# Storing an image once in four row bands and gathering it by rows of taps, and making two rank masks once, in a one-core kernel with four layers

## Chip, cores and metric

The kernel runs on one core of one Trainium2 chip, in one launch. Its metric is the device time in microseconds (us). The kernel before took 10140.57 us (median of three runs, 10136.91 to 10153.51). One more execution was profiled. It took 10153.48 us, of which 10151.7 us lie between its first and its last instruction.

## What is computed

The reference is a stack of four layers on a float32 tensor x of shape (4, 128, 64, 64): four images of 128 channels. Only layer 0 is touched, and in it only the part that ends with the order of the patches:

```
x_adapted = gn(x)
feat = gelu(dwconv2d(x_adapted, conv1_w, conv1_b))     # 3x3, each channel alone
ca = feat.mean((2, 3))
ca = sigmoid(maximum(ca @ ca1_w.T, 0.0) @ ca2_w.T)
feat = feat * ca[:, :, None, None]
feat = gelu(dwconv2d(feat, conv2_w, conv2_b))          # 3x3, each channel alone
scores = sigmoid(einsum('bchw,oc->bohw', feat, head_w)[:, 0] + head_b[0])
pv = var(x_adapted, axis=1, ddof=1)
final_scores = 0.7 * scores + 0.3 * sigmoid(pv * 10.0)
sm = final_scores.reshape(B, Hp, PS, Wp, PS).mean((2, 4)).reshape(B, Hp * Wp)
idx = argsort(-sm, axis=1)                             # 256 patches of 4x4 pixels
```

The patches in this order, with a position embedding added and normalized, go through a projection, a causal convolution, a selective scan over the 4096 positions (16 states, 256 inner channels) and a projection back. Layer 1 is a 3x3 convolution over all channels. Layers 2 and 3 are an attention and a small mixture of experts each, and the change does not touch them.

## The kernel before

`layers01` holds layers 0 and 1. It has three stages, each with its own pools.

Stage one prepares image 0: it runs the generator `in_order(0)` alone, on engines that are otherwise empty. Stage two is `scan`: it goes through the four images, eight chunks of 512 positions each and eight pairs of states (g) in each chunk. For each g, VectorE (DVE) makes `hs` (L901) and runs four scans (L912) with `decay` factors that ScalarE (ACT) computes just ahead (L908), in two half turns of two scans each. GpSimd (POOL) multiplies `hs` by `c_sb` (L916), which SyncE (SP) loads from DRAM (L870), and TensorE (PE) adds it up (`y_ps`). Beside this, `scan` advances `in_order(b + 1)` by one turn (one `yield`) in every half turn, so that image b + 1 is prepared while image b is scanned. In the last image's scan, the finished images go through layer 1 instead (`end`). Stage three finishes the last image.

Stage one is ordered by the tile framework's scheduler. In stage two the order on each engine is the order in which the program writes the instructions (`manual_schedule`). All engines take their instructions in order; so a wait at the head of one engine's queue holds up what is behind it. Operations handed to `later` are written at the next `flush`, which is half a turn later.

All DMAs of the kernel are issued by SP. In the built program a DMA also waits, before it is issued, until the DMA eight places ahead of it on SP has landed: there are eight semaphores, used in rotation.

How one image gets its two depthwise convolutions (lines of the kernel before):

- `groupnorm_fill` (L209) writes eight rows of `xp`, the normalized image with a border of zeros: 128 channels by 66 rows by 66 columns.
- `stored(img, i, half)` (L438) writes the image to DRAM, to `image_d[i]`, which is laid out as [4, 96, 64 x 66]: four groups of 32 channels, and for each group three copies of its channels, shifted by 0, 1 and 2 rows (the three rows ky of the filter). One half of an image takes twelve DMAs of 264 KB (L444): four groups by three shifts, 32 partitions each.
- `gather(i, c)` (L451) reads what eight rows of output need into `under`, a tile of 96 partitions (3 ky by 32 channels) by 4 groups by 528 elements, with one DMA of 792 KB (L454). There are two such buffers, so gather c + 2 waits on SP until the convolution of c has read its buffer.
- `convolved` (L460) makes one chunk with 12 groups of matmuls, which contract over the 96 partitions (`conv<-under,deep` in the profile).
- `first(c)` applies Gelu on ACT and writes the result to `fp`, a bordered image as well. `fp` is then stored and gathered in the same manner for the second convolution (`second`, L528), whose chunks also need `ca`, the gate from the mean of all of `fp`, and have more work: the channel variance (`pv_mean`, `pv_sq`), the head product and a tanh (`gauged`, `two`, `two_t`).

`staged` runs these steps in a pipeline, with a new chunk every two turns. A chunk is gathered in one turn and convolved three turns later. The first half of `xp` is stored once seven of its eight parts are filled, the second half after all. `fp` is stored in halves after its chunks 4 and 7 (`first_stored`, L499).

`sort` (L568) turns the 256 scores `sm` into ranks. For each half h of the patches it makes `dg` and `cl` (the scores as a column), then `before` (L582: which column number lies above the row's own number, from `K.col` and `K.row`), `eq` (L584: equal scores, taken only where `before` is 1) and `beats` (L586). A matmul adds up `beats` to the rank.

Of the kernel before, what the change touches and what calls it, by code (L numbers as in the profile page):

```python
# [9 lines left out]
F32 = mybir.dt.float32  # L10
# [3 lines left out]
ALU = mybir.AluOpType  # L14
# [3 lines left out]
P = 128  # L18
NB = 4
HW = 64  # L20
# [9 lines left out]
class Common:  # L30
# [59 lines left out]
    def mm(self, out, lhsT, rhs, start=True, stop=True):  # L90
        self.nc.tensor.matmul(out, lhsT, rhs, start=start, stop=stop)  # L91
# [32 lines left out]
    def later(self, f, *args, **kw):  # L124

        self.late.append(lambda: f(*args, **kw))
# [144 lines left out]
def layers01(K, xd, dpool, w, w1):  # L271
# [3 lines left out]
    nc, tc, mm = K.nc, K.tc, K.mm  # L275
# [5 lines left out]
    with ExitStack() as ctx:  # L281
# [3 lines left out]
        small = pool("l0_small", 1)  # L285
# [16 lines left out]
        for z in range(2):  # L302
            for q in range(NQ):
                nc.sync.dma_start(
                    out=a_neg[64 * z : 64 * z + 64, q, :].unsqueeze(2),
                    in_=w["A_log"][64 * q : 64 * q + 64, :].rearrange("d (g z) -> d g z", z=2)[:, :, z : z + 1],
# [9 lines left out]
        for at, rows_ in ((0, slice(0, 24)), (64, slice(24, 40))):  # L316
            nc.sync.dma_start(
                out=x_projT[:, :, at : at + rows_.stop - rows_.start],
                in_=w["x_proj_wT"].rearrange("(k p) f -> p k f", k=2)[:, :, rows_],
# [3 lines left out]
        state = cst.tile([32, DS], F32, name="state")  # L323
        nc.vector.tensor_scalar(state, K.col[0:32, 8 : 8 + DS], row32[0:32], None, ALU.is_equal)
        c_d = dpool.tile([2, DS, CH], F32, name="c_d")
        image_d = [dpool.tile([4, 96, HW * (HW + 2)], F32, name=f"image_d{i}") for i in range(2)]
        y_d = [dpool.tile([P, L], F32, name=f"y_d{b}") for b in range(NB - 2)]

        pair = cst.tile([P, 64], F32, name="pair")
# [47 lines left out]
        deep2 = depthwise(w["conv2_w"], "deep2")  # L377
        rect = lambda t: t.rearrange("p (y x) -> p y x", x=HW)
        ones256 = K.ones[:, 0:1].to_broadcast([P, 256])

        def image(b):
            t = big.tile([P, L], F32, name="xb", tag="mid")
            src = w["x"][b].rearrange("c h w -> c (h w)")
            for q in range(4):
                at = slice(q * L // 4, (q + 1) * L // 4)
                nc.sync.dma_start(out=t[:, at], in_=src[:, at])
            return t
# [28 lines left out]
        def wait(n):  # L416
            for _ in range(n):
                yield
# [5 lines left out]
        def in_order(b, made, work, psum):  # L424
# [5 lines left out]
            xp = big.tile([P, HW + 2, HW + 2], F32, name="xp", tag=f"seq{b % 2}")  # L430
# [4 lines left out]
            sm = small.tile([P, 256], F32, name="sm")  # L435
            unders, kept, squares, features, xls = {}, {}, {}, {}, {}

            def stored(img, i, half):  # L438


                n = HW // 2 * (HW + 2)
                for g in range(4):
                    for ky in range(3):
                        nc.sync.dma_start(  # L444
                            out=image_d[i][g, 32 * ky : 32 * ky + 32, n * half : n * half + n],
                            in_=img[32 * g : 32 * g + 32, HW // 2 * half + ky : HW // 2 * (half + 1) + ky, :].rearrange(
                                "p y x -> p (y x)"
                            ),
                        )

            def gather(i, c):  # L451
                n = 8 * (HW + 2)
                t = unders[c] = work.tile([96, 4, n], F32, name="under", bufs=2)
                nc.sync.dma_start(out=t, in_=image_d[i][:, :, n * c : n * c + n].rearrange("g q f -> q g f"))  # L454

            def even():
                while K.slot % 2:
# [27 lines left out]

            for c in range(NCH):
                fill(c)
                if c == 6:
                    stored(xp, 0, 0)
                yield  # L490
            fp = kept["fp"] = big.tile([P, HW + 2, HW + 2], F32, name="fp", tag="mid")
            nc.gpsimd.memset(fp[:, 0, :], 0.0)
# [1 line left out]
            nc.gpsimd.memset(fp[:, 1 : HW + 1, 0:1], 0.0)  # L494
            nc.gpsimd.memset(fp[:, 1 : HW + 1, HW + 1 : HW + 2], 0.0)
            yield
            stored(xp, 0, 1)

            def first_stored(c):  # L499
                if c in (4, 7):  # L500
                    stored(fp, 1, c // 5)

            yield from even()
            yield from staged(NCH, 2, lambda c: gather(0, c), None, None, first, None, first_stored)

            def attention_of_channels():
# [17 lines left out]
            def gather_second(c):  # L524
                gather(1, c)
                begun[0] += 1
# [41 lines left out]
            def sort():  # L568
                yield from wait(6)
                sp = K.bank(psum, [P, 256], "sm_ps")  # L570
                mm(sp, share.to_broadcast([P, P]), sm)
                later(nc.vector.tensor_copy, sm, sp)
                yield from wait(2)
                beats = []
                for h in range(2):
                    dg = small.tile([P, P], F32, name="dg")
                    nc.vector.tensor_tensor(dg, sm[:, h * P : (h + 1) * P], K.ident, ALU.mult)
                    cl = small.tile([P, 1], F32, name="cl")
                    nc.vector.tensor_reduce(cl, dg, AX.X, ALU.add)

                    before = small.tile([P, 256], F32, name="before")
                    nc.vector.scalar_tensor_tensor(before, K.col, K.row[:, h : h + 1], ones256, ALU.is_gt, ALU.mult)  # L582
                    eq = small.tile([P, 256], F32, name="eq", tag="rank_eq")
                    nc.vector.scalar_tensor_tensor(eq, sm, cl, before, ALU.is_equal, ALU.mult)  # L584
                    bt = small.tile([P, 256], F32, name=f"beats{h}")
                    nc.vector.scalar_tensor_tensor(bt, sm, cl, eq, ALU.is_lt, ALU.add)  # L586
                    beats.append(bt)
                    yield
                yield
                rp = K.bank(psum, [P, 256], "rank_ps")  # L590
                for h in range(2):
                    mm(rp, K.ones, beats[h], start=h == 0, stop=h == 1)
                rank = small.tile([P, 256], F32, name="rank", bufs=NB)
                kept["rank"] = rank
                later(nc.vector.tensor_copy, rank, rp)
                yield
                yield
                for h in range(2):
                    dg = small.tile([P, P], F32, name="dg")
                    nc.vector.tensor_tensor(dg, rank[:, h * P : (h + 1) * P], K.ident, ALU.mult)  # L600
                    cl = small.tile([P, 1], F32, name="cl")
                    nc.vector.tensor_reduce(cl, dg, AX.X, ALU.add)
                    pm = small.tile([P, 256], F32, name=f"perm{h}", tag=f"beats{h}")
                    nc.vector.scalar_tensor_tensor(pm, K.col, cl, ones256, ALU.is_equal, ALU.mult)
                    perm.append(pm)
                    yield
# [74 lines left out]
            def backs():  # L681
                for n in range(NCH):
# [3 lines left out]
                    yield from wait(2 if n < 4 else 1)  # L686

            yield from together(tail, sort(), staged(NCH, 2, ask, None, placed, centred, None, varied), backs())
            yield

# [341 lines left out]
        with (  # L1032
            tc.tile_pool(name="l0_first", bufs=2) as work,
            tc.tile_pool(name="l0_ps", bufs=8, space=PSUM) as psum,
        ):
            for K.slot, _ in enumerate(in_order(0, seqs, work, psum)):
                K.flush()
            K.flush()
# [972 lines left out]
@with_exitstack  # L2011
def kernel(ctx: ExitStack, tc: tile.TileContext, w: dict, out: bass.AP):
    nc = tc.nc
    cpool = ctx.enter_context(tc.tile_pool(name="const", bufs=1))
    dpool = ctx.enter_context(tc.tile_pool(name="dram", bufs=1, space=bass.MemoryType.DRAM))
    K = Common(tc, cpool)

    def of(prefix):
        return {k[len(prefix) :]: v for k, v in w.items() if k.startswith(prefix)}

    xd = [dpool.tile([P, L], F32, name=f"xd{b}") for b in range(NB)]
    layers01(K, xd, dpool, {"x": w["x"], **of("L0_conv_")}, of("L1_conv_"))
    layer2_attention(K, xd, dpool, of("L2_attn_"))
    xpool = ctx.enter_context(tc.tile_pool(name="x", bufs=1))
    xs = []
    for b in range(NB):
        t = xpool.tile([P, L], F32, name=f"x{b}")
        nc.sync.dma_start(out=t, in_=xd[b])
        xs.append(t)
    expert_ffn(K, xs, of("L2_ffn_"), "f2")  # L2030
    layer3_attention(K, xs, of("L3_attn_"))
    expert_ffn(K, xs, of("L3_ffn_"), "f3")
    for b in range(NB):
        nc.sync.dma_start(out=out[b].rearrange("c h w -> c (h w)"), in_=xs[b])
# [54 lines left out]
```

## Times and profile before

| | us |
|---|---|
| Runs: median (lowest to highest) | 10140.57 (10136.91 to 10153.51) |
| Profiled execution, whole | 10153.48 |
| Its span, first to last instruction | 10151.7 |
| of this, stage one (image 0 prepared, to the first scan) | 0 to about 281 |
| of this, stage two (scan) | about 281 to about 2754 |
| PE, DVE, ACT, POOL busy over the span | 8749.1, 7495.5, 7369.4, 4792.9 |
| DMA: moved in all | 669.32 MB |
| `image_d<-xp` and `image_d<-fp`, 96 DMAs of 264 KB each | 51.9 MB |
| `under<-image_d`, 64 DMAs of 792 KB | 51.9 MB |

A line of a timeline gives the start in us, the duration in us, the engine, the line of the kernel, the operation, the written tile and what it reads, the shape, the number of merged instructions (x), and in brackets how long the engine sat idle before it and what released it. `SPq` is SP's queue: its durations are the time that SP spent on issuing DMAs, not the transfers. A line of the windows gives for a stretch (us from the span's start) its length, the busy us and the instructions of PE, PEld (weight loads), DVE, ACT and POOL, then the granted TensorE clock, the mean busy share of the DMA engines, and GB/s moved.

### The profile page before, as it was taken

The numbers are of one execution on the slowest core, as the hardware profiler recorded it, in microseconds if no ns is written. First come the engines' busy times: TensorE is split into PE (matmuls) and PEld (weight loads), VectorE is DVE, ScalarE is ACT, GpSimd is POOL, SyncE is SP. The second block draws the span as 40 slices with busy tenths as digits, with TensorE's granted clock in tenths as the row PEclk, the third lists the DMA queues.
The fourth block names the chain that finished last, engine by engine and source line by source line (L and its number), as shares of the span: only waits on it lengthen the run. The fifth ranks groups of instructions, "written<-read, shape, count | busy, mean of one in ns | idle before, by whom it ended". The sixth has DMA issues, their size and how long they took to land. (4 is left out here: it accounts for less than half of the span.)

```text
span 10151.7 us, 186504 instructions
## 1 busy us (share of the span) xinstructions
PE 8749.1 (86%) x72920; PEld 3331.9 (33%) x72920; DVE 7495.5 (74%) x8191; ACT 7369.4 (73%) x10574; POOL 4792.9 (47%) x3135
## 2 busy tenths in 40 slices
PE   5687787889859999969999979999979999967766
PEld 2122222234433333323333333333323333323433
DVE  1779797887748888778888778888778888753563
ACT  2666766654439999869999869999869999841531
POOL 0567586765525555445555445555445555420000
PEclk9787887889979999989999989999989999988988
DMA  5634536322221222141222142222142222123004
GB/s 126 146 90 105 125 81 149 71 68 78 73 70 35 41 38 39 29 113 36 41 38 40 30 111 37 39 39 40 34 107 38 39 39 39 38 92 118 0 18 150
DMA packets 629618, 669.32 MB, mean 66 GB/s; under 512 B 185400, under 2 KB 416896, under 8 KB 621568
## 3 DMA queue, kind: packets, MB, share of 16 engines
q1 hardware_dynamic: 628736, 657.39, 28.4%
q8 instruction: 575, 9.42, 0.4%
q14 instruction: 307, 2.51, 0.1%
HBM read 446.84 MB, written 143.13 MB: 58 GB/s over the span
## 5 line engine op out<-in xcount | busy, mean ns | idle before, releaser
L1506 ACT ACTIVATE ex<-score 128x1024 f32<-128x1024 f32 x5120 | 4925.0, 1036 | 179.4 <-PE score L91 90.1
L91 PE MATMUL ctx_ps<-ex,qt 128*32 128x512 f32 x20480 | 2735.3, 606 | 20.0 <-DVE ctx L1440 20.0
L1455 POOL TENSOR_TENSOR folded<-ex 128x1024 f32<-128x1024 f32 x512 | 1224.0, 2391 | 2125.1 <-ACT ex L1506 1869.9
L1512 DVE STREAM_TRANSPOSE turned<-ex 128x1024 f32<-128x1024 f32 x1536 | 1885.0, 1227 | 377.1 <-ACT ex L1506 296.1
L1488 DVE STREAM_TRANSPOSE turned<-ex 128x1024 f32<-128x1024 f32 x1532 | 1841.5, 1202 | 0.0
L91 PE MATMUL acc_ps<-turned,turned_v 128*32 128x256 f32 x24576 | 1769.5, 379 | 3.0 <-DVE turned L1518 3.0
L912 DVE TENSOR_TENSOR_SCAN hs<-decay,carry,hs 128x512 f32<-128x512 f32 x1024 | 1245.2, 1264 | 251.2 <-ACT decay L908 238.2
L91 PE MATMUL score<-queries,keys 32*128 32x512 f32 x10240 | 1335.3, 497 | 96.5 <-ACT ex L1506 44.1
L91 PEld LDWEIGHTS acc_ps<-turned,turned_v 128*32 128x32 f32 x24576 | 800.9, 110 | 1476.4 <-issue 1327.1
L916 POOL TENSOR_TENSOR hs<-hs,c_sb 128x1024 f32<-128x1024 f32 x512 | 1207.1, 2358 | 113.2 <-DMA c_sb<-c_d 73.0
L908 ACT ACTIVATE decay<-dt,a_neg 128x512 f32<-128x512 f32 x1024 | 692.8, 689 | 656.6 <-DVE hs L912 645.8
L91 PEld LDWEIGHTS score<-queries,keys 32*128 32x128 f32 x10240 | 513.5, 182 | 1193.5 <-ACT ex L1506 819.3
L1312 POOL TENSOR_TENSOR turned_v<-v,quarter 128x1024 f32<-128x1024 f32 x256 | 612.5, 2393 | 266.0 <-PE acc_ps L91 223.4
L91 PE MATMUL y_ps<-hs,pair 128*64 128x512 f32 x2048 | 657.8, 769 | 30.3 <-POOL hs L916 29.9
L1456 POOL TENSOR_TENSOR quarters<-folded 128x512 f32<-128x512 f32 x512 | 657.7, 1285 | 40.2
L901 DVE TENSOR_TENSOR hs<-dtx,b_ps 128x2048 f32<-128x2048 f32 x256 | 579.8, 2265 | 65.3 <-PE b_ps L91 35.8
L91 PEld LDWEIGHTS ctx_ps<-ex,qt 128*32 128x32 f32 x20480 | 406.4, 108 | 655.4 <-issue 599.3
L91 PE MATMUL b_ps<-dbc,state 32*64 32x512 f32 x1024 | 341.0, 748 | 226.6 <-DVE hs L901 226.2
L1506 ACT ACTIVATION_READ_ACCUMULATOR ex<-score 128x1 f32 x2048 | 436.6, 213 | 0.0
L915 POOL COPY carry<-hs 128x2 f32<-128x2 f32 x512 | 97.9, 191 | 713.4 <-DVE hs L912 682.9
L1440 DVE COPY ctx<-ctx_ps 128x512 f32<-128x512 f32 x256 | 176.8, 691 | 329.5 <-PE ctx_ps L91 318.9
L91 PE MATMUL conv<-under,deep 96*32 96x512 f32 x1536 | 218.7, 710 | 143.0 <-DMA under<-image_d 142.9
(361 smaller groups left out, 9349.5 us busy)
## 6 DMA issues: line engine op xcount, KB each, us to landing
c_sb<-c_d SPq DMA_DIRECT2D x512, 128.0 KB
queries<-head_d SPq DMA_DIRECT2D x1024, 64.0 KB
keys<-head_d SPq DMA_DIRECT2D x1024, 64.0 KB
under<-image_d SPq DMA_DIRECT2D x64, 792.0 KB
dt<-dt SPq DMA_DIRECT2D x128, 256.0 KB
dtx<-dtx SPq DMA_DIRECT2D x128, 256.0 KB
v<-value_d SPq DMA_DIRECT2D x1024, 32.0 KB
w<-in_L_ffn_weight SPq DMA_DIRECT2D x32, 1024.0 KB
```

What stands on the lines that cost most here:

```text
L91: self.nc.tensor.matmul(out, lhsT, rhs, start=start, stop=stop)
L901: nc.vector.tensor_tensor(hs, dtx2, bb.unsqueeze(1).to_broadcast([P, NQ, CH]), ALU.mult)
L908: nc.scalar.activation(ex, dt2[:, q, :], AF.Exp, scale=a_neg[:, q, g : g + 1])
L912: nc.vector.tensor_tensor_scan(hs[:, q, :], decays[q - 2 * i], hs[:, q, :], carry[:, g, q : q + 1], ALU.mult, ALU.add)
L916: nc.gpsimd.tensor_tensor(hs[:, two, :], hs[:, two, :], cs.unsqueeze(1).to_broadcast([P, 2, CH]), ALU.mult)
L1312: nc.gpsimd.tensor_tensor(t, v.unsqueeze(2).to_broadcast([P, 4 * BT, 4, HD]), quarter.unsqueeze(1).to_broadcast([P, 4 * BT, 4, HD]), ALU.mult,
L1440: nc.vector.tensor_copy(u, cps)
L1455: nc.gpsimd.tensor_tensor(hs, exs[:, :, 0], exs[:, :, 1], ALU.add)
L1456: nc.gpsimd.tensor_tensor(qs, hs[:, :, 0 : CH // 2], hs[:, :, CH // 2 :], ALU.add)
L1488: nc.vector.transpose(*upright)
L1506: nc.scalar.activation(ex, sps[p], AF.Exp, scale=scale, accum_out=sums[:, t : t + 1] if summed else None)
L1512: nc.vector.transpose(*upright)
```

## The change

`image_d[i]` becomes [128, 66 x 66]: the bordered image once, without copies. `stored` takes a quarter q, and writes rows 0 to 16, 17 to 32, 33 to 48 or 49 to 65 of all 128 channels with one DMA (561 KB for the outer, 528 KB for the inner quarters). `gather` takes three DMAs instead of one, one for each ky, which read the same rows shifted by ky and write 32 partitions of `under` each (264 KB). The stores are written earlier: those of `xp` after fills 3, 5 and 7 and once more after the memsets of `fp`; those of `fp` after chunks 1, 3, 5 and 7. The two `before` masks, one for each half, are made once at the start and kept, and `eq` reads them.

```
-        image_d = [dpool.tile([4, 96, HW * (HW + 2)], F32, name=f"image_d{i}") for i in range(2)]
+        image_d = [dpool.tile([P, (HW + 2) * (HW + 2)], F32, name=f"image_d{i}") for i in range(2)]
...
+        befores = [small.tile([P, 256], F32, name=f"before{h}", bufs=1) for h in range(2)]
+        for h in range(2):
+            nc.vector.tensor_scalar(befores[h], K.col, K.row[:, h : h + 1], None, ALU.is_gt)
...
-            def stored(img, i, half):
-                n = HW // 2 * (HW + 2)
-                for g in range(4):
-                    for ky in range(3):
-                        nc.sync.dma_start(
-                            out=image_d[i][g, 32 * ky : 32 * ky + 32, n * half : n * half + n],
-                            in_=img[32 * g : 32 * g + 32, HW // 2 * half + ky : HW // 2 * (half + 1) + ky, :].rearrange(
-                                "p y x -> p (y x)"
-                            ),
-                        )
+            def stored(img, i, q):
+                lo, hi = 16 * q + 1 if q else 0, 16 * q + 17 if q < 3 else HW + 2
+                nc.sync.dma_start(
+                    out=image_d[i][:, lo * (HW + 2) : hi * (HW + 2)], in_=img[:, lo:hi].rearrange("p y x -> p (y x)")
+                )
             def gather(i, c):
                 n = 8 * (HW + 2)
                 t = unders[c] = work.tile([96, 4, n], F32, name="under", bufs=2)
-                nc.sync.dma_start(out=t, in_=image_d[i][:, :, n * c : n * c + n].rearrange("g q f -> q g f"))
+                for ky in range(3):
+                    at = (8 * c + ky) * (HW + 2)
+                    nc.sync.dma_start(
+                        out=t[32 * ky : 32 * ky + 32],
+                        in_=image_d[i][:, at : at + n].rearrange("(g q) f -> q g f", q=32),
+                    )
...
             for c in range(NCH):
                 fill(c)
-                if c == 6:
-                    stored(xp, 0, 0)
+                if c in (3, 5, 7):
+                    stored(xp, 0, c // 2 - 1)
                 yield
...
-            stored(xp, 0, 1)
+            stored(xp, 0, 3)
             def first_stored(c):
-                if c in (4, 7):
-                    stored(fp, 1, c // 5)
+                if c % 2:
+                    stored(fp, 1, c // 2)
...
-                    before = small.tile([P, 256], F32, name="before")
-                    nc.vector.scalar_tensor_tensor(before, K.col, K.row[:, h : h + 1], ones256, ALU.is_gt, ALU.mult)
                     eq = small.tile([P, 256], F32, name="eq", tag="rank_eq")
-                    nc.vector.scalar_tensor_tensor(eq, sm, cl, before, ALU.is_equal, ALU.mult)
+                    nc.vector.scalar_tensor_tensor(eq, sm, cl, befores[h], ALU.is_equal, ALU.mult)
```

In the built program, ACT's and POOL's instructions stand in the same order before and after, and PE's and DVE's too, but for two places: the two masks move to the start, and in stage one the scheduler exchanges one `two` matmul with its neighbour and one transpose with its neighbours. SP's order differs in the stores and gathers alone, with 192 stores and 64 gathers before, and 32 stores and 192 gathers after.

## Prediction

> **What bounds the kernel now.** I read the windows first. Where image 0 is prepared alone, they show which engine works at all:
>
> ```profile
> 37.00:65.00 28.00, 0.00 (x0) 0.00 (x0) 0.00 (x0) 2.58 (x4) 0.55 (x5) 1.00 0.95 214
> 65.00:110.00 45.00, 25.71 (x168) 6.01 (x168) 0.00 (x0) 6.73 (x15) 0.00 (x0) 0.92 0.77 192
> 110.00:150.00 40.00, 21.77 (x98) 5.19 (x102) 1.69 (x4) 8.54 (x13) 0.00 (x0) 0.73 0.85 201
> 150.00:190.00 40.00, 38.94 (x200) 9.36 (x192) 4.95 (x9) 14.79 (x23) 0.26 (x1) 0.93 0.37 90
> ```
>
> From 37 to 65 us PE, the first number after the length, has nothing to do, and the DMA engines are 95% busy at 214 GB/s. Only after 150 us is PE full. SP's queue tells with what, and PE's timeline what it costs:
>
> ```profile
> 36.83 28.00 SPq L444 DMA_DIRECT2D image_d<-xp  x24
> 64.88 26.90 SPq L454 DMA_DIRECT2D under<-image_d  x6
> ...
> 98.79 12.47 SPq L444 DMA_DIRECT2D image_d<-fp  x11
> ...
> 126.47 13.65 SPq L444 DMA_DIRECT2D image_d<-fp  x12
> ```
>
> ```profile
> 74.20 8.61 PE L91 MATMUL conv<-under,deep 96*32 96x512 f32 x48 [41.09 <-DMA under<-image_d]
> ...
> 120.56 5.05 PE L91 MATMUL conv<-under,deep 96*32 96x512 f32 x24 [12.00 <-DMA under<-image_d]
> ...
> 149.08 5.35 PE L91 MATMUL conv<-under,deep 96*32 96x512 f32 x24 [6.06 <-DMA under<-image_d]
> ```
>
> 24 stores of 264 KB keep SP for 28 us, since each waits for the one eight places ahead. PE gets its first gather at 74.20. The stores of `fp` make gaps at 120 and 149.
>
> In the scan DVE bounds: it is busy 368.16 of 398 us where image 1's later steps run (592 to 990), but 138.84 of 206 us beside its convolutions (386 to 592). Why, SP, PE and DVE show in turn:
>
> ```profile
> 486.95 3.08 SPq L804 DMA_DIRECT2D dtx<-dtx  x4
> 490.13 13.37 SPq L444 DMA_DIRECT2D image_d<-fp  x12
> 503.55 2.63 SPq L870 DMA_DIRECT2D c_sb<-c_d  x2
> 506.29 0.54 SPq L454 DMA_DIRECT2D under<-image_d  x1
> ```
>
> ```profile
> 513.74 4.72 PE L91 MATMUL conv<-under,deep 96*32 96x512 f32 x24 [11.70 <-DMA under<-image_d]
> ```
>
> ```profile
> 410.06 2.46 DVE L912 TENSOR_TENSOR_SCAN hs<-decay,carry,hs 128x512 f32<-128x512 f32 x2 [11.06 <-ACT decay L908]
> 418.08 2.46 DVE L912 TENSOR_TENSOR_SCAN hs<-decay,carry,hs 128x512 f32<-128x512 f32 x2 [0.82 <-ACT decay L908]
> 430.86 2.46 DVE L912 TENSOR_TENSOR_SCAN hs<-decay,carry,hs 128x512 f32<-128x512 f32 x2 [5.58 <-ACT decay L908]
> 522.69 2.46 DVE L912 TENSOR_TENSOR_SCAN hs<-decay,carry,hs 128x512 f32<-128x512 f32 x2 [17.02 <-ACT decay L908]
> ```
>
> The stores hold SP 13.4 us, the gather behind them lands late, PE waits 11.70 us, ACT (in order, Gelu ahead of the next `decay`) waits 14.95 us, and DVE stands still for 17.02 us. So the name on DVE's line, ACT, is not the cause; the DMA is. 418.08 is a convolution whose data was there: 0.82 us.
>
> **The skill, and the trace.** (1) "DMA: Bandwidth & Descriptors", Two DMAs through the same engine are not ordered: a DMA that reads what another wrote must wait for that one's semaphore. The trace agrees: PE's first convolution comes only after all 24 stores. In the built program after, gather 0 waits for quarter 0 alone, gather 1 for quarter 1 too. (2) "SBUF — State Buffer", Door 1: partitions 0 to 31 reach half of the ports, 189 GB/s at 1 MiB, about 218 at best. The trace: stores out of 32 partitions took 28.00/24 = 1.17 us for 264 KB (270,336 bytes), 231 GB/s, somewhat over that. No row shows a large load into 32 partitions. (3) The same page, The DMA setup-cost knee: some 2 us fixed for each DMA. Here four `dt` DMAs (1 MB), issued from 268.81 on, released ACT's last wait at 274.67: 5.9 us, or 4.9 at 214 GB/s and 1 more. I take 1.5, between the two. (4) The same page, Who interferes with whom: a DVE instruction with two inputs in SBUF is blocked while a GpSimd instruction reads SBUF. The trace agrees, see the masks below.
>
> **Stores, stage one.** One store of an image falls from 6.49 MB (24 x 270,336 bytes) to 2.23 MB (128 x 4356 x 4 bytes).
> - First convolution: before, 7.30 MB with gather 0 until 74.20. After, quarter 0 needs only fills 0 and 1 (fills take 0.72 us from 33.84 on), so it goes out at 35.3; 2.23 + 0.81 MB at 214 GB/s are 14.2 us, with 0.4 to issue and 1.5 to land: 51.4. Gain 22.8.
> - Its eight chunks take 51.4 us before (74.20 to 125.6). After, DMA sets the pace: seven more gathers at 3.8 us and three stores of `fp` at 2.6 are 34.4, and 4 for the last chunk: 38.4. Gain 13.0.
> - The first chunk of the second convolution follows its gate at 128.92 without a wait now. After, it waits for the fourth store and a third of its gather: loss 3.5.
> - The rest of the second convolution: PE needs 5.8 us a chunk (157.68 to 163.48) and gathers take 3.8, so it is PE's. Lost is the gap at 149.08 (6.06) and a cold clock (5.35 instead of 2.78 us): gain 8.6.
> The sum is 40.9. Following the DMAs one by one with 200 GB/s, 2 us and 4.5 us a chunk gives 31, with 230 GB/s and warm chunks 45. I take 40. Nothing else is late next: `pos_xc`, at 185.63 now, follows the second convolution, and no other engine has work there.
>
> **Stores, scan.** In images 1, 2 and 3 the stalls behind stores are 11.06 + 5.58, 7.32 + 2.03 and 8.40 + 5.94 us at the first gathers, and 17.02, 17.48 and 18.02 at the second convolution: 92.9. What stays: at the first, 1.5 for each of six (0.82 as at 418.08, and some DMA queue): 9. At the second, `dtx` (1.05 MB from 487 on), the store, two pairs of `c_sb` (0.26 MB each) and the gather are 2.96 MB, 13.8 us, landing at 502.3 with the 1.5, where PE could start at 502.0 (513.74 less 11.70): I count 1, and for ACT's table loads and Gelu 3.7 (as the stall at 544.75): 4.7 for each of three, 14. Gain 70. The gather of chunk 7 behind `fp`'s first half costs ACT 1.05 us at 481.23: 3 in three images. Next late is ACT, whose stalls of 2 to 4 us from 544 to 599 stay.
>
> The new stores are four DMAs, not 24, each issued turns after its rows are made; ahead of `c_sb` they cost SP about 0.4 us each, or 2.6 where the queue is full. A store of `fp` can make SP wait for ACT's Gelu; behind it stand `c_sb`, and POOL behind that, which has 2 us of slack per g (two times 2.54 of 7.1).
>
> **Gathers.** Two more DMAs for each, at some 0.42 us (0.31 and the 0.1 between): 0.85 us for 48 gathers in the scan, 41 us of SP's time. SP has cover: it waits 323.9 us for `carry` ahead of `dt` alone up to 1950. Of it I count 5 us; without this cover it would be up to 30. Below nothing is excluded, since the bytes are the same. For the rate I take 214 GB/s; the page's 189 would make 4.3 us out of 3.8, and adds 4 in stage one.
>
> **Masks.** Six L582 in the scan take 2.5 us, as the profile has it:
>
> ```profile
> 633.29 2.52 DVE L582 SCALAR_TENSOR_TENSOR before<-col,row,ones 128x256 f32<-128x256 f32 x1
> 635.84 1.29 DVE L584 SCALAR_TENSOR_TENSOR eq<-sm,cl,before 128x256 f32<-128x256 f32 x1
> ```
>
> ```profile
> 633.18 2.35 POOL L916 TENSOR_TENSOR hs<-hs,c_sb 128x1024 f32<-128x1024 f32 x1
> ```
>
> It is tempting to count 6 x 2.5 = 15 us. But L582 takes 0.47 us alone (stage one) and here ends when POOL does (635.53). Without it, `eq`, also with two inputs in SBUF, meets the same POOL instruction. Gain 0.45 x 6 = 2.7, with 0 and 15 as the ends. The two masks at the start (about 0.3 us each) are hidden by DVE's wait for constants and x until 20 us.
>
> **Sum.** 40 + 70 + 3 + 2.7 - 5 = 110.7. Against the profiled execution, 10153.48 (span 10151.7 and 1.8 around it), that is 10042.8; this execution stood 12.9 above the median. The median, 10140.57, becomes 10029.9; I say 10030. Layers 2 and 3 keep their orders and count 0; a PE clock granted differently may move them by some us.
>
> **Rivals.**
> - Stage one gains, the scan hardly: ACT's table loads and DMA traffic of `dt` and `dtx` take the place of the waits. For it: second convolutions whose data was there still stall 3.7. Against: 418.08 and 530.18 (0.94). 35 + 20: 10085.
> - More is gained: smaller stalls next to the convolutions go too, since 206 us at 386 to 592 hold 18 g that need 7.1 to 8.2 elsewhere, 59 us more at best for each image. Half as much again in the scan: 10140.6 - 155 = 9985.
> - Slower: the three-part gathers run at a much lower rate into 32 partitions. At r GB/s each of 64 takes 811/r us. Stage one exposes 16, where the convolutions become DMA-bound at 7 us or more; in the scan a gather has some 8 us (two half turns) with 0.6 MB of other loads (2.8 us) beside it. At 100 GB/s a gather takes 8.1: 16 x 4.3 = 69 in stage one, 48 x (8.1 + 2.8 - 8 = 2.9) = 139 in the scan, less 111: 10240. It decides from about 140 GB/s downwards. Against: 231 GB/s for stores of the same 32 partitions.
> - That the change does not do what it says: the built order excludes it, with 4 stores and 24 gather DMAs for each image.
>
> **Numbers.** Forecast (70 to 135 us gained) 0.68, scan hardly gains 0.13, more gained 0.12, slower 0.06, no visible change 0.01. The range, 9980 to 10090, leaves out the slower case, the little change, and the ends of the two cases beside the forecast, some 0.15 in all. Faster by over 0.2% (20 us, about what a measurement of this kernel can tell from no change) 0.93, same 0.01, slower 0.06.
>
> **What would show it.** DMA in all falls from 669.32 to about 635.3 MB (8 x 4.26 less). The first `conv` on PE at 49 to 56 us, `pos_xc` at 141 to 155. No store holds SP for 13 us. In the scan, no stall of DVE above 6 us beside the convolutions. L584 takes 2.5 us where L582 did. I am wrong if a gather alone takes over 5 us to land, if `conv` still waits for `under` by 5 us and more, or if DVE's stalls stay while PE's are gone.

## The result and the profile after

The changed kernel took 10038.47 us (median of four runs, 10030.25 to 10047.85), the kernel before, run beside it, 10138.74 (10134.09 to 10153.51). The ratio is 0.9899, with a 95% interval from 0.9882 to 0.9916: about 100 us less. The forecast was 10030. The profiled execution took 10030.25 us, with a span of 10028.5. It was the fastest of the four, and the profiled one of before was as slow as the slowest of its runs, so these two lie 123 us apart.

The page first: what the DMA engines moved (before: 669.32 MB; forecast: 635.3).

```profile
DMA packets 627058, 635.26 MB, mean 63 GB/s; under 512 B 184888, under 2 KB 416384, under 8 KB 625152
```

The windows of stage one, with the columns as before:

```profile
37.00:65.00 28.00, 14.26 (x96) 3.82 (x96) 0.00 (x0) 5.37 (x11) 0.51 (x4) 1.00 0.87 213
65.00:110.00 45.00, 36.71 (x192) 9.21 (x192) 1.69 (x4) 12.15 (x21) 0.00 (x0) 0.81 0.71 170
110.00:150.00 40.00, 36.91 (x198) 9.65 (x196) 11.18 (x23) 18.56 (x29) 3.56 (x3) 1.00 0.43 99
150.00:190.00 40.00, 28.71 (x181) 22.68 (x180) 8.58 (x17) 17.05 (x28) 16.94 (x20) 0.87 0.05 14
```

From 37 to 65 us PE now works for 14.26 us, where it had nothing to do; from 65 to 150 it is busy for 36.71 of 45 and 36.91 of 40 us, and after 150 the DMA engines are all but idle. SP's queue and PE's timeline there:

```profile
33.81 4.51 SPq L445 DMA_DIRECT2D image_d<-xp  x4
38.41 17.07 SPq L454 DMA_DIRECT2D under<-image_d  x12
```

```profile
45.47 8.70 PE L91 MATMUL conv<-under,deep 96*32 96x512 f32 x48 [13.97 <-DMA under<-image_d]
...
89.80 5.35 PE L91 MATMUL conv<-under,deep 96*32 96x512 f32 x24 [2.07 <-DMA under<-image_d]
```

Four stores take the place of 24, and the first convolution starts at 45.47, not 74.20. The only gap that is new is the one at the start of the second convolution, 89.80.

In the scan of image 1, the last store ahead of the second convolution on SP, and then three stalls of DVE: at chunks 0 and 1 of the first convolution, and at the start of the second:

```profile
436.38 0.76 SPq L445 DMA_DIRECT2D image_d<-fp  x1
```

```profile
351.42 2.46 DVE L913 TENSOR_TENSOR_SCAN hs<-decay,carry,hs 128x512 f32<-128x512 f32 x2 [1.06 <-ACT decay L909]
...
366.57 2.46 DVE L913 TENSOR_TENSOR_SCAN hs<-decay,carry,hs 128x512 f32<-128x512 f32 x2 [7.95 <-ACT decay L909]
...
455.78 2.46 DVE L913 TENSOR_TENSOR_SCAN hs<-decay,carry,hs 128x512 f32<-128x512 f32 x2 [4.92 <-ACT decay L909]
```

The last store of `fp` holds SP for 0.76 us instead of 13.37, and the stall that follows is 4.92 us instead of 17.02. The stall at chunk 0 of the first convolution fell from 11.06 to 1.06. But chunk 1, which did not stall before (0.82), now stalls for 7.95.

Where the time went, from the two traces (the scan from the start of the first `hs` of L901, now L902, to the start of the last):

| | before | after | gained | forecast |
|---|---|---|---|---|
| Stage one, to the first `hs` | 281.10 | 232.44 | 48.7 | 40 |
| Scan | 2464.8 | 2406.5 | 58.3 | 70.7 |
| Last `hs` to the end of the span | 7405.8 | 7389.6 | 16.2 | 0 |

The last row is code that the change does not touch. A second execution of the same changed kernel (e4 below) took 7402.3 us there, 12.7 more than the first, so that row is not put down to the change. What is left for the change in the profile is 107.0 us, where the sum said 110.7.

### The profile page after: what moved, and what is told of

Same layout as the page of the kernel before. It is cut to its first block, busy times and chain, and to the rows that moved or that the text cites. A ratio compares the mean times of both kernels' runs of the same rounds, so it can differ in the third digit from the quotient of the medians.

```text
span 10028.5 us, 186542 instructions
## 1 busy us (share of the span) xinstructions
PE 8716.9 (87%) x72920; PEld 3321.5 (33%) x72920; DVE 7494.2 (75%) x8185; ACT 7372.6 (74%) x10574; POOL 4793.8 (48%) x3135
## 5 line engine op out<-in xcount | busy, mean ns | idle before, releaser
L902 DVE TENSOR_TENSOR hs<-dtx,b_ps 128x2048 f32<-128x2048 f32 x256 | 580.5, 2268 | 62.8 <-PE b_ps L91 32.7
L1498 DVE TENSOR_REDUCE dacc<-quarters 128x2 f32<-128x512 f32 x508 | 327.4, 645 | 0.0
```

The costliest lines, as they stand in the source:

```text
L902: nc.vector.tensor_tensor(hs, dtx2, bb.unsqueeze(1).to_broadcast([P, NQ, CH]), ALU.mult)
L1498: nc.vector.tensor_reduce(at, qs, AX.X, ALU.add)
```

## Experiments

The kernel before ran beside each group of them; its medians were 10145.79 (e1 to e4), 10148.76 (e5 to e8) and 10143.76 (e9, e10). Since the last part of the span moves by over 10 us for no reason in the code, small effects are read from the trace: the start of the scan and its length.

| | median us (range) | ratio [95%] | stage one | scan |
|---|---|---|---|---|
| e1, before with masks once | 10138.07 (10129.15 to 10156.47) | 0.9997 [0.9989, 1.0005] | 283.5 | 2.9 less than before |
| e2, bands at the old points | 10062.23 (10055.23 to 10065.77) | 0.9917 [0.9904, 0.9931] | 238.2 | 2413.5 |
| e3, chunk 1 with chunk 0 | 10029.70 (10026.44 to 10032.88) | 0.9886 [0.9871, 0.9901] | 238.7 | 2392.6 |
| e4, the changed kernel again | 10042.50 (10037.87 to 10053.15) | 0.9900 [0.9886, 0.9914] | 234.0 | 2406.7 |
| e5, each band stored three times | 10085.78 (10078.70 to 10087.11) | 0.9941 [0.9926, 0.9956] | 255.1 | 2423.8 |
| e6, six DMAs for a gather | 10045.10 (10043.67 to 10050.46) | 0.9903 [0.9888, 0.9918] | 231.8 | 2403.3 |
| e7, all gathers earlier | 10035.59 (10022.74 to 10043.13) | 0.9891 [0.9872, 0.9910] | 232.5 | 2390.1 |
| e8, e3 again | 10032.18 (10026.72 to 10040.64) | 0.9890 [0.9875, 0.9905] | 233.4 | 2391.3 |
| e9, bands stored by 32 partitions | 10049.05 (10043.79 to 10050.77) | 0.9904 [0.9890, 0.9919] | 239.7 | 2402.9 |
| e10, e3 with convolutions first on PE | 10043.13 (10039.67 to 10048.81) | 0.9900 [0.9884, 0.9917] | 232.4 | 2406.3 |

**e1: the masks alone.** The kernel before, with the two masks made once.

```
-                    nc.vector.scalar_tensor_tensor(before, K.col, K.row[:, h : h + 1], ones256, ALU.is_gt, ALU.mult)
-                    nc.vector.scalar_tensor_tensor(eq, sm, cl, before, ALU.is_equal, ALU.mult)
+                    nc.vector.scalar_tensor_tensor(eq, sm, cl, befores[h], ALU.is_equal, ALU.mult)
```

> The kernel before with the masks made once, stores and gathers as before. Theory (the wait for GpSimd's reads moves from the removed instruction to the next one with two inputs in SBUF): the three rank instructions that follow each other take some 3.6 us less in the three images of the scan, the time falls by about 3 us, to 10136 where before has 10139, no difference that the times can tell, and the `eq` instructions take 2.4 us where they took 0.5 to 1.3. Rival (each removed instruction's 2.5 us is gained): 15 us less, 10124.

No difference in time can be measured, and the trace has a scan that is 2.9 us shorter. Single places elsewhere in this scan differ from before by up to 3.7 us either way, so it is the six places themselves that tell: 0.51 to 0.53 us each, 3.1 in all. So 15 us for six removed instructions of 2.5 us falls. This is how the changed kernel looks there, on DVE and on POOL:

```profile
567.10 2.39 DVE L585 SCALAR_TENSOR_TENSOR eq<-sm,cl,before 128x256 f32<-128x256 f32 x1
```

```profile
566.87 2.34 POOL L917 TENSOR_TENSOR hs<-hs,c_sb 128x1024 f32<-128x1024 f32 x1
```

`eq` ends at 569.49, just behind POOL's end at 569.21. It has inherited the 2.4 us of the instruction that is gone.

**e2: the layout alone.** The changed kernel, its bands stored in pairs where the halves were stored before.

```
-                if c in (3, 5, 7):
-                    stored(xp, 0, c // 2 - 1)
+                if c == 6:
+                    stored(xp, 0, 0)
+                    stored(xp, 0, 1)
...
-                if c % 2:
-                    stored(fp, 1, c // 2)
+                if c in (4, 7):
+                    stored(fp, 1, c // 5 * 2)
+                    stored(fp, 1, c // 5 * 2 + 1)
```

> The changed kernel, but its four bands are stored in pairs at the points where the kernel before stored its halves (after fill 6 and at the end; after chunks 4 and 7). Theory (bytes on the DMA queue and the number of stores that hold SP are what counts): the scan keeps at least 45 of its 58 us, the stage of image 0 loses a little (the first band leaves after fill 3 at the earliest), the time is 10040 to 10055. Rival (storing early and in bands is what counts): most is lost, 10090 and more, and the first gather of the scan's images lands late again, with stalls of over 6 us at the first and at the ninth convolution.

It keeps 43 of the 49 us of stage one and 51 of the 58 of the scan. The median lies 20 us above e4's, more than the theory had: 11 of them are in these two stages, the rest lies in untouched code. The earlier points of storing are thus the smaller part of the change; the image stored once is the larger.

**e3 and e8: the gather of chunk 1 ahead of `dt`.** This tests why chunk 1 stalls now. SP's queue in the changed kernel around it, then PE:

```profile
325.25 1.47 SPq L454 DMA_DIRECT2D under<-image_d  x3
345.52 3.63 SPq L805 DMA_DIRECT2D dt<-dt  x4
349.19 1.66 SPq L871 DMA_DIRECT2D c_sb<-c_d  x2
350.90 1.57 SPq L454 DMA_DIRECT2D under<-image_d  x3
```

```profile
359.03 4.66 PE L91 MATMUL conv<-under,deep 96*32 96x512 f32 x24 [4.06 <-DMA under<-image_d]
```

After gather 0, SP stands until 345.52, because the next DMA in the program is `dt`, which POOL has not made yet. Gather 1 is behind it, and then behind its 1 MB on the way: it is issued at 350.90 and its convolution starts at 359.03. In the kernel before, chunk 0 stalled for 11 us at this place, and gather 1, issued at 398.99, had landed by its turn. The edit issues it with gather 0:

```
+            def gather_first(c):
+                if c != 1:
+                    gather(0, c)
+                if c == 0:
+                    gather(0, 1)
```

> The changed kernel, with the gather of chunk 1 of the first convolution issued in the turn of chunk 0's, ahead of the dt transfers on SP. Theory (in the changed kernel the stall that was at chunk 0 stands at chunk 1, because its gather is queued behind dt, whose turn SP waits for on POOL): the stalls of 7.95, 7.26 and 6.45 us at chunk 1 fall to 2 or less, and the time falls by 10 to 18 us against the changed kernel, to 10020 to 10030. Rival (the transfers of dt and dtx fill the DMA engines just then): the stalls stay or move on to chunk 2, and the time is that of the changed kernel within 5 us.

> The changed kernel itself, beside the others on the same chip: 10030 to 10048 by every theory, about 100 us below before.

> The version that fetches chunk 1 with chunk 0, once more, beside the one that fetches all of them earlier. Theory: 10025 to 10033 us, and its stage one, 6 us longer than the changed kernel's in the first execution, is within 2 us of it this time, since the difference came with the granted clock and the later x. Rival: stage one is 4 to 8 us longer again, since the gather of chunk 1 now stands ahead of the last stores: then the gain of an early gather is the scan's alone and a version that does it in the scan only would be better.

The scan gets 14 to 15 us shorter in both executions (2392.6 and 2391.3 against 2406.5 and 2406.7), and the time 12.8 less than e4's beside it. The two intervals overlap, so the gain rests on the scan's length, which repeats within 1.3 us. Stage one was longer in e3 alone: in e8 it is 233.4, within a microsecond of the changed kernel's. SP, PE and DVE in e8:

```profile
326.18 3.17 SPq L454 DMA_DIRECT2D under<-image_d  x6
```

```profile
353.95 1.98 PE L91 MATMUL y_ps<-hs,pair 128*64 128x512 f32 x4 [2.48 <-POOL hs L923]
355.86 4.99 PE L91 MATMUL conv<-under,deep 96*32 96x512 f32 x24
```

```profile
363.74 2.46 DVE L919 TENSOR_TENSOR_SCAN hs<-decay,carry,hs 128x512 f32<-128x512 f32 x2 [4.20 <-ACT decay L915]
```

Chunk 1's convolution no longer waits for `under`. But 4.20 us of the 7.95 are left, although the data is there. In images 2 and 3 chunk 1's stall falls further, from 7.26 and 6.45 us to 0.51 and 2.28, but chunk 2's rises there, from 1.63 and 0.80 to 4.29 and 3.85.

What is left at chunk 1 goes with PE's clock. Its convolution in images 1, 2 and 3 of e8, in the columns of the windows (the granted clock is third from the end):

```profile
355.86:360.85 4.99, 4.99 (x28) 1.07 (x28) 3.58 (x3) 0.97 (x1) 4.00 (x3) 0.55 1.07 223
937.48:940.26 2.78, 2.78 (x28) 0.74 (x28) 2.67 (x3) 1.98 (x2) 2.70 (x3) 1.00 1.08 211
1518.44:1522.41 3.97, 3.97 (x28) 0.91 (x28) 3.87 (x3) 1.85 (x2) 3.89 (x3) 0.69 1.07 210
```

PE's order is the same in all three, and `y_ps`, just ahead, waits 2.48, 1.91 and 2.03 us for POOL. Yet the stall left is 4.20 us where the convolution took 4.99, 0.51 where it took 2.78, and 2.28 where it took 3.97. Between images 1 and 2 the stall differs by 3.69 us; 2.21 of them are the slower convolution and 0.90 the slower `y_ps` ahead of it (1.98 us for 1.08).

**e7: every gather of the first convolution earlier.** I took the stalls that were left in e3 (4.19, 4.13 and 3.81 us) for chunk 2 and its gather in all three images.

```
+            def gather_next(c):
+                if 0 < c < NCH - 1:
+                    gather(0, c + 1)
+            yield from staged(NCH, 2, gather_first, gather_next, None, first, None, first_stored)
```

> The version that fetches chunk 1 with chunk 0, and besides fetches every later chunk of the first convolution one turn earlier than it does, as soon as the convolution two chunks back is issued. Theory (the stall that was left at chunk 2, 4.2, 4.1 and 3.8 us in the three images, is again a gather that stands behind dtx on SP): these stalls go, 5 to 12 us less than that version, 10018 to 10026. Rival (the earlier gather makes SP wait for PE, and c_sb and dtx stand behind it): no gain or a loss, 10030 to 10050.

The theory falls in image 1: the stall is still 4.16 us (at 363.86), it belongs to chunk 1, and no gather makes it. In images 2 and 3 it holds: chunk 2's stalls, 4.29 and 3.85 us in e8, are down to 0.11 and 0.14. Still the scan is only 1.2 us shorter than e8's, since stalls grew elsewhere, the largest at chunk 1 of image 2: 4.16 us for 0.51, with a convolution of 4.73 us at a granted clock of 0.58 for one of 2.78 at 1.00.

**e10: convolutions ahead of the sum on PE.** The other suspect for the 4.20 us is PE's order. What stands in front of the convolution at 355.86 is `y_ps`, which waits 2.48 us for POOL. Here it is written behind:

```
-                            if past is not None:
+                            if past is not None and (g == 0 or b + 1 == NB):
                                 add(*past)
...
+                        if i == 1:
+                            if g and b + 1 < NB:
+                                add(*past)
+                            past = n, g, hs
```

> The version that fetches chunk 1 with chunk 0, with one change of PE's order in the scan of images 0 to 2: in a half turn that has both, the products of the next image (convolutions among them) are written ahead of the sum y_ps, which waits for POOL. Theory (what is left of DVE's stall at chunk 1, 4.2 us in the first image, is PE's y_ps waiting 2.5 us for POOL in front of a convolution whose data has landed): the convolution comes 3 to 4 us earlier, that stall falls below 1.5 us, and those at the second convolution, 4.75 us in the first image, fall by up to 3: 10 to 30 us less than that version, 10000 to 10022. Rival A (it is ACT's change of table and Gelu, or the gather): the stall stays above 3.5 us and the time at 10025 to 10035. Rival B (y_ps comes later, holds hs and POOL, and DVE waits for those): slower, above 10040.

The convolution moves forward, the gain doesn't come. PE and DVE:

```profile
350.07 2.78 PE L91 MATMUL conv<-under,deep 96*32 96x512 f32 x24
...
364.99 4.96 PE L91 MATMUL conv<-under,deep 96*32 96x512 f32 x24 [8.84 <-DMA under<-image_d]
```

```profile
372.83 2.46 DVE L919 TENSOR_TENSOR_SCAN hs<-decay,carry,hs 128x512 f32<-128x512 f32 x2 [7.91 <-ACT decay L915]
```

Chunk 1 is convolved 5.8 us earlier (1.0 of it since the scan began earlier) and DVE doesn't stall for it. But it also had the full clock here (2.78 us), as in image 2 of e8, where the old order left only 0.51 us; so e10 does not show that the order was the cause. Now chunk 2 comes before its data, which is queued behind `dtx` (1 MB): 7.91 us there. Over the scan, 15 us are lost against e8, some 13 of them in the second convolutions. Their first chunks took 5.22, 5.35 and 5.35 us on PE in the three images, at granted clocks of 0.52, 0.50 and 0.50, where e8's took 2.78 at 1.00, and the stalls behind them are 6.45, 6.39 and 6.30 us for 4.75, 4.70 and 3.66. Rival B had the sign and the size, but its mechanism is not what stands there: at chunk 2 it is the gather, and at the second convolutions a PE that has waited 1.95 to 3.47 us for the gather and then runs slowly. Whether the new order brings the lower clock was not tested.

**e5: the bytes back, without their waits.** Each band is written to two spare images too.

```
+                for d in (image_d[i], spare_d[2 * i], spare_d[2 * i + 1]):
+                    nc.sync.dma_start(
+                        out=d[:, lo * (HW + 2) : hi * (HW + 2)], in_=img[:, lo:hi].rearrange("p y x -> p (y x)")
+                    )
```

> The changed kernel, with every band written two more times, to spare DRAM images that nobody reads: an image is 12 DMAs and 6.69 MB again, about the bytes of the kernel before (6.49 MB), but no gather waits for the spare writes by a semaphore. Theory (in stage one bytes decide, in the scan what holds SP and stands ahead of a gather): stage one loses (2 x 4.46 MB at 270 GB/s = 33 us) less some 8 that lie beside PE, 25; the scan loses at most 15, since the writes are spread over the turns: 10060 to 10090 us. Rival, bytes are the whole cause: what the stores gained, about 100 us, is lost, 10130 to 10145. Rival, bytes are nothing and the count of DMAs and their place is all: 10035 to 10050.

10085.78: 47 us above the changed kernel. Stage one loses 22.6 (25 expected), 1.6 of them by an `xp` that was ready later; its first convolution on PE:

```profile
58.48 8.51 PE L91 MATMUL conv<-under,deep 96*32 96x512 f32 x48 [25.38 <-DMA under<-image_d]
```

The scan loses 17.3, a little over the 15 expected, nearly all of it at the start of the second convolutions, the one place where a store stands right ahead of a gather that PE waits for:

```profile
479.72 2.46 DVE L915 TENSOR_TENSOR_SCAN hs<-decay,carry,hs 128x512 f32<-128x512 f32 x2 [8.32 <-ACT decay L911]
```

8.32 us for 4.92; in the other two images these places lose 8.5 and 7.8 us, some of which comes back elsewhere. So with the bytes of before, the scan still keeps 41 of its 58 us. There the bytes were the smaller cost; the larger, by this reading, was the 12 stores at one point of SP's queue, each waiting for the one eight places ahead. This is argued and not shown, since the extra bytes also move faster than the stores of before: at 375 GB/s from 35 to 52 us (I had reckoned with 270), where those went at 214. In stage one the bytes count, for the same reason, for at least about half: 22.6 of 48.7.

**e6: twice as many DMAs for the gathers.**

```
+                    for z in range(2):
                         nc.sync.dma_start(
-                            out=t[32 * ky : 32 * ky + 32],
+                            out=t[32 * ky : 32 * ky + 32, :, z * n // 2 : (z + 1) * n // 2],
```

> The changed kernel with each of the three row gathers cut in two by columns: six DMAs of 135 KB for a chunk instead of three of 270 KB, the same bytes. 144 more DMAs in the scan, at about 0.42 us of SP each 60 us of SP's time, and 48 in stage one, 20 us. Theory (SP has cover for issue in the scan, and stage one is set by bytes): 0 to 12 us slower than the changed kernel, 10040 to 10055. Rival (issue on SP, or the wait for the DMA eight places ahead, is exposed wherever a convolution waits): 35 to 80 us slower, 10075 to 10120.

Nothing is lost that can be measured: stage one and scan are 0.7 and 3.2 us shorter than in the changed kernel. SP's time for issuing is covered.

**e9: bands stored by 32 partitions.** Same bytes, four DMAs for each band.

```
+                for g in range(4):
+                    p = slice(32 * g, 32 * g + 32)
                     nc.sync.dma_start(
+                        out=image_d[i][p, lo * (HW + 2) : hi * (HW + 2)], in_=img[p, lo:hi].rearrange("p y x -> p (y x)")
                     )
```

> The changed kernel with each band stored by four DMAs of 32 partitions instead of one of 128: the same bytes and places, 16 store DMAs for an image instead of 4. Theory (a store out of 128 partitions moves at about 400 GB/s, one out of 32 at about 231, as in the kernel before): image 0's four bands take 2.23 MB / 231 = 9.7 us instead of 5.6, so PE's first convolution comes 3 to 6 us later than in the changed kernel, at 48.5 to 51.5; in the scan 36 more DMAs from SP and slower stores cost 0 to 12 us; 10042 to 10062. Rival (the rate is that of an otherwise empty DMA system, whatever the partitions): the first convolution stays within 1.5 us of 45.5.

GB/s in 40 equal slices of 33 to 60 us, first of the changed kernel, then of e9:

```profile
GB/s 0 0 259 386 400 419 376 400 386 412 266 188 275 219 216 235 210 238 207 200 197 203 16 0 0 0 0 22 150 344 207 200 235 207 253 200 200 225 230 368
```

```profile
GB/s 0 0 0 0 0 206 206 286 228 313 288 238 294 244 263 273 279 205 260 250 216 194 250 260 238 200 200 241 72 3 0 0 0 0 28 153 338 203 194 247
```

Stores out of 128 partitions go at 376 to 419 GB/s; the gathers behind them, into 32 partitions each, at 188 to 275. For these the partitions are not the reason: one gather of before went into 96 partitions, and moved 211 GB/s (65 to 73 us) where the three-part ones move 219 (40.5 to 47.8). Stored by 32 partitions, the bytes of the bands go at 206 to 313, 253 on average from 36.2 to 44. The first convolution comes at 50.18, inside the range of the theory; but `xp` was 1.9 us late in that execution (first fill at 34.12, not 32.23), so 2.8 us of the 4.7 are the partitions', a little less than the 3 to 6 expected. The scan is 3.6 us shorter than the changed kernel's, so the slower stores cost nothing there.

## Why the prediction was right, and where it was not

**The bound and the main mechanism** were right: DVE's stalls named ACT, and came from stores at the head of SP's queue. (That PE's first convolution came only after all 24 stores, which I took as agreeing with the rule that two DMAs are not ordered, shows no more than SP's order: gather 0 stood behind all of them there.) The group of all convolutions on PE, before and after (busy, mean ns, idle time and what ended it):

```profile
L91 PE MATMUL conv<-under,deep 96*32 96x512 f32 x1536 | 218.7, 710 | 143.0 <-DMA under<-image_d 142.9
```

```profile
L91 PE MATMUL conv<-under,deep 96*32 96x512 f32 x1536 | 200.2, 659 | 46.2 <-DMA under<-image_d 39.0 <-ACT decay L909 4.1 <-ACT fp L126 3.1
```

104 us of waiting for `under` are gone.

**Stage one** was mis-sized: 48.7, outside my 31 to 45. Its terms: first convolution 28.7 (22.8 said); the eight chunks 13.0 (13.0); the first chunk of the second convolution -2.6 (-3.5); its rest 8.1 (8.6); to the first `hs` 1.5 (none said). The failed term is the first. "2.23 + 0.81 MB at 214 GB/s" used one rate for two things: 214 was that of stores out of 32 partitions. The new stores leave from 128, and took some 5.6 us at 400 GB/s, not 10.4. The Trainium skill says so in the same table that I cited for the gathers ("SBUF — State Buffer", Door 1: partitions 0 to 127 reach all 16 ports, 328 GB/s at 1 MiB and 436 at best, with twice the ports that 0 to 31 reach); e9 agrees, though its 253 GB/s lie above the 218 that the table gives 32 partitions at best. Another 1.6 us came from an `xp` that was ready sooner in this execution (32.23, not 33.84), which is no effect of the change. So two of my signs were passed on the early side: the first convolution at 45.47 (49 to 56 said), `pos_xc` at 138.44 (141 to 155).

**Stores, scan.** At the second convolutions I said 52.5 less 14; it is 52.5 less 13.5 (4.92, 4.84, 3.71). Chunk 7: 3 said, 2 found. At the first gathers I said 40.3 less 9, "1.5 for each of six", and only 14.5 came, taken from one `hs` of L901 to the next: 5.1 in image 1, nothing in image 2, 9.6 in image 3. This is the step that failed: I priced what stays by chunk 1 of before, which was quiet because its data had landed while chunk 0 stalled, and which ran at the full clock (2.78 us). Now chunk 1 stalls for 7.95, 7.26 and 6.45 us in the three images. In image 1, 3.75 us of that are its gather behind `dt` (e8). Of the 4.20 that stay, most go with a PE at a granted clock of 0.55, as images 1 and 2 of e8 show side by side; why the clock was low there stays open. Of my two signs against it, "no stall of DVE above 6 us" failed, and rightly told that something had moved. "If a gather alone takes over 5 us to land" was not met: this one took 8.1, but not alone.

**Gathers, SP.** I counted a loss of 5, up to 30. e6 doubles them and loses nothing that can be measured, so the term is 0 within some 3 us.

**Masks.** 2.7 said, 3.1 at the six places in e1. `eq` took 2.39 to 2.43 us where I said 2.5. The Trainium skill's page "SBUF — State Buffer", Who interferes with whom, is borne out once more: the next instruction with two inputs in SBUF waits for POOL in place of the one removed.

**The sum.** Stage one was 9 too low, the scan 12 too high; 107.0 in the profile for 110.7 is close by luck, because the two errors have opposite signs. Rival "slower by the gathers": their rate, 188 to 275 GB/s, is well above the 140 where it begins. Rival "more is gained": the small stalls at later chunks stayed (3.73 us at 477.85 for 3.72 at 544.75). Rival "the scan hardly gains" held in one place of three, the first gathers, with `dt` as it said.

## What to carry to other kernels

Where a stall disappears, look at what stood behind it and was quiet: it may have been served by the stall, so price it from a place where nothing waited. In a queue that is served in order, a load that could go goes ahead of one that must wait for another engine: moving one gather ahead of `dt` gives 14 to 15 us of the scan, and that version, with medians of 10030 and 10032 us, is the fastest here. Take a store's rate from one with the same number of partitions, not from the stores that it replaces; for the gathers of this kernel the partitions made no difference. And before a stall that is left is put down to the order of the instructions, compare the granted clock at the same place in another image.

## What the runs showed of the hardware

Three things. Stores by 32 partitions, with several in flight, reached 313 GB/s in single slices and 253 on average (e9), more than the 231 of the kernel before; those out of 128 partitions stayed near 400. Gathers moved 211 GB/s into 96 partitions and 219 into 32; what limits them is not shown.

The length of a convolution of 24 matmuls follows the granted clock: 2.78 us at 1.00, 4.66 at 0.59 (359.03 above) and 5.35 at 0.50 (89.80). A low clock often stands behind a wait of PE, but not only there. In the scan of the kernel before, all ten chunks before which PE had been idle for over 2 us took more than 3 us, and 4 of the other 38; in e10 all five, and 12 of the other 43. And in stage one of the changed kernel two chunks took 2.78 us right after waits of 2.82 and 2.83 us (at 56.99 and 77.47). So a wait for `under` can be followed by some 2 us of slower work, but what sets the clock is not settled here.
